# Routed feed-forward block: two plain indexed writes and a gather in place of one adding write per row

## The chip, the cores and the metric

The kernel runs on one core of a Trainium2 chip. The metric is the device time of one execution in microseconds. Before the change, three runs gave 889.02, 889.24 and 949.13 us; the median is 889.24.

## The reference, cut to what matters

One layer over four sequences of 512 tokens with 256 values each. First a conditioned feed-forward block and an attention with 16 heads on one shared key and value; their result is added to the input. Then a per-sequence mixed linear map and a routed feed-forward block with eight experts, again added:

```python
x = x + attn(cond(x, cond_8, ...), ...)
x = x + ffn(cond2(x, cond_8, ...), w_router, wi, wo)

def ffn(x, w_router, wi, wo):                       # x as 8 groups of 256 tokens
    dispatch, combine = _routing(xg, w_router)      # a token goes to its 2 best of 8 experts,
                                                    # at most 128 rows per group and expert
    expert_in = einsum('gth,gtec->gech', xg, dispatch)
    h = gelu(einsum('gech,ehf->gecf', expert_in, wi))
    expert_out = einsum('gecf,efh->gech', h, wo)
    out = einsum('gech,gtec->gth', expert_out, combine)   # weighted by the router's probability
```

So an output row is the residual of its token plus up to two expert rows, each times its probability. All arithmetic is in 32-bit floats.

## The kernel before

**Stages.** Weights of the conditioned block are gathered by row index and applied; attention runs as a software pipeline over 64 steps (16 per sequence); the pieces of the finished sequence before it (`finish`) are put between the steps one by one. The pieces of `finish(b)` end with the routing: `out` adds the attention's result to the input, giving the residual `r`, and writes it to `out_rows` (L435); `mix` makes the rows `x3` that the experts read; `choose` takes each token's two best experts; `places` gives every chosen row its place in a table `xp` in device memory, sorted by expert, and writes the rows there by eight indexed DMAs per sequence (L570), 32 in all. A row of `x3` and `xp` carries 256 values and four numbers more: the token number plus one (zero in a row that nobody filled), the first choice's expert, and both probabilities. `xp` is filled with zeros once, near the start (L199).

**The routed stage.** The last stage runs over 39 tiles of 128 rows of `xp` (`NTILE`), as many as the eight experts can need with their last tiles partly filled. Small VectorE operations work out the expert of each tile (`texp`) and its first row. The loop over tiles issues, per turn: `up(t)`, `fetch_in(t + 3)`, `turn(t + 1)`, `put(t - 1)`, `fetch_out(t + 2)`.

- `fetch_in` loads on SP's queue the tile's rows, `xt` (four buffers, L662), and the expert's first weights, `wi` (1 MB, three buffers, L671). `fetch_out` loads the second weights, `wo` (1 MB, three buffers, L675).
- `turn` transposes the rows on TensorE into PSUM (L681) and VectorE copies them to `xT` (L683).
- `up` multiplies by `wi` (L691, 32 matmul instructions in the profile); ScalarE applies the gelu (L695).
- `put` multiplies by `wo` (L704, 16 instructions) into one PSUM bank `po`. VectorE works out each row's weight and the row of the output that it belongs to, `at` (L712 to L718; a row that nobody filled goes to one of 128 spare rows behind the output), scales the row into `y` (L720), and POOL issues an indexed DMA that adds `y` to those rows of `out_rows` (L721).

**What sets the order.** The order on each engine is the order of the program; no planner moves instructions. Waits come from a dependency tracker: a reader waits for the writer of what it reads, a writer for the readers and the writer of what it overwrites. Two DMAs on `out_rows` count as conflicting, so each L721 waits for the L721 before it. Buffers in turn (`at`, `w0`, `w1` and `y` have two each) make a write wait for the last reader two tiles earlier, and for `at` and `y` that reader is a DMA. A tile's `xt` buffer is free when its last reader on VectorE is done. The rows of `xp` are declared free of conflict among themselves ("rows"); the first load of `xt` waits for all 32.

Of the kernel before, what the change touches and what calls it, by code (L numbers as in the profile page):

```python
# [9 lines left out]
F32 = mybir.dt.float32  # L10
I32 = mybir.dt.int32
AF = mybir.ActivationFunctionType
ALU = mybir.AluOpType
# [3 lines left out]
P = 128  # L17
B = 4
T = 512
NT = B * T  # L20
D = 256
NE = 8
# [4 lines left out]
CAP = 128  # L27
# [2 lines left out]
NCH = NT // P  # L30
EROWS = NG * CAP
NTILE = 2 * NCH + NE - 1
XROW = D + 4
WROW = 3 * 1024 + 10


# [1 line left out]
def adaln_attn_ffn_kernel(  # L38
# [22 lines left out]
    nc = tc.nc  # L61
# [33 lines left out]
    rows = const.tile([P, B], I32, name="rows")  # L95
    top = const.tile([P, B], F32, name="top")
    first = const.tile([P, B, NE], F32, name="first")
# [22 lines left out]
    for b in range(B):  # L120
# [3 lines left out]
            out=w,  # L124
            out_offset=None,
            in_=wcond,
            in_offset=bass.IndirectOffsetOnAxis(ap=rows[:, b : b + 1], axis=0),
# [6 lines left out]
    def load(ap, shape, name):  # L134
# [22 lines left out]
        out=upto, in_=ones, compare_op=ALU.is_ge, fill=0.0, base=0,  # L157
# [6 lines left out]
        out=sel, in_=sel, compare_op=ALU.not_equal, fill=1.0, base=-HD,  # L164
# [5 lines left out]
    for hg in range(4):  # L170
        nc.gpsimd.affine_select(
            out=spread, in_=spread, compare_op=ALU.not_equal, fill=1.0, base=-32 * hg,
            pattern=[[-1, 4], [0, 32]], channel_multiplier=1,
        )
    def numbers(name, shape, pattern, base, step):
        t = const.tile(shape, F32, name=name)
        nc.gpsimd.iota(
            t, pattern=pattern, base=base, channel_multiplier=step,
            allow_small_or_imprecise_dtypes=True,
        )  # L180
        return t


    token1 = numbers("token1", [P, NCH], [[P, NCH]], 1, 1)
    spare1 = numbers("spare1", [P, 1], [[0, 1]], NT + 1, 1)

    free = numbers("free", [P, NE], [[EROWS, NE]], 0, 0)
    begin = numbers("begin", [P, NE, NG], [[EROWS, NE], [P, NG]], 0, 0)
# [197 lines left out]
    def finish(b):  # L386

        s = seqs[b]
# [30 lines left out]
        def out(cc):  # L419

            def piece():
                if cc == 0:
                    s["r"] = rp.tile([P, 4, D], F32, name="r", bufs=1)
                px = bank(psC, "psC")
                for n in range(2):
                    for hg in range(4):
                        mm(  # L427
                            px[:, ts(n, D)], s["attn"][:, hg, ts(2 * cc + n, P)], wo_sb[:, hg, :],
                            start=hg == 0, stop=hg == 3,
                        )  # L430
                r2 = s["r"][:, ds(2 * cc, 2), :]
                nc.vector.tensor_tensor(
                    r2, px.rearrange("p (n d) -> p n d", n=2), s["x"][:, ds(2 * cc, 2), :], ALU.add
                )
                nc.sync.dma_start(  # L435
                    out_rows[ds(b * T + 2 * cc * P, 2 * P), :].rearrange("(n p) d -> p n d", p=P),
                    r2,
                )
            return piece
# [13 lines left out]

        def mix(cc):
            def piece():
                if cc == 0:
                    s["x3"] = rp.tile([P, 4, XROW], F32, name="x3")
                px = bank(psC, "psC")
                for n in range(2):
                    for c in range(2):  # L460
                        mm(
                            px[:, ts(n, D)], s["rT"][:, c, ts(2 * cc + n, P)], wb[:, c, :],
                            start=c == 0, stop=c == 1,
                        )
                nc.vector.tensor_tensor(
                    s["x3"][:, ds(2 * cc, 2), 0:D], px.rearrange("p (n d) -> p n d", n=2),
                    bias2_sb.unsqueeze(1).to_broadcast([P, 2, D]), ALU.add,
                )
            return piece

        def small(name, shape=(P, 4, NE)):
            return rp.tile(list(shape), F32, name=name)
# [4 lines left out]
        def choose():  # L477

            pl = bank(psC, "psC")
            for ch in range(4):  # L480
                for c in range(2):
                    mm(
                        pl[:, ts(ch, NE)], s["x3T"][:, c, ts(ch, P)], wr_sb[:, c, :],
                        start=c == 0, stop=c == 1,
                    )
            lg = pl[:, 0 : 4 * NE].rearrange("p (c e) -> p c e", c=4)
            rev_b = rev.unsqueeze(1).to_broadcast([P, 4, NE])
            m = small("m", (P, 4))
            nc.vector.tensor_reduce(m, lg, AX.X, ALU.max)
            pr = small("pr")  # L490
            nc.vector.tensor_tensor(pr, lg, over_experts(m), ALU.subtract)
            nc.scalar.activation(pr, pr, AF.Exp)
            sm = small("sm", (P, 4))
            nc.vector.tensor_reduce(sm, pr, AX.X, ALU.add)
            nc.vector.reciprocal(sm, sm)
            nc.vector.tensor_tensor(pr, pr, over_experts(sm), ALU.mult)

            hot = small("hot", (P, 2, 4, NE))
            top2 = small("top2", (P, 2, 4))
            left = pr  # L500
            for k in range(2):
                mk = small(f"mk{k}", (P, 4))
                nc.vector.tensor_reduce(top2[:, k], left, AX.X, ALU.max)  # L503
                eq = small(f"eq{k}")
                nc.vector.tensor_tensor(eq, left, over_experts(top2[:, k]), ALU.is_equal)
                nc.vector.tensor_tensor(eq, eq, rev_b, ALU.mult)
                nc.vector.tensor_reduce(mk, eq, AX.X, ALU.max)
                nc.vector.tensor_tensor(hot[:, k], rev_b, over_experts(mk), ALU.is_equal)
                if k == 0:
                    left = small("left")  # L510
                    nc.vector.scalar_tensor_tensor(
                        left, hot[:, 0], -4.0, pr, ALU.mult, ALU.add
                    )
                    nc.vector.tensor_scalar(
                        s["x3"][:, :, D + 1], mk, -1.0, float(NE), ALU.mult, ALU.add
                    )
            nc.gpsimd.tensor_copy(s["x3"][:, :, D], token1[:, ts(b, 4)])
            nc.gpsimd.tensor_copy(  # L518
                s["x3"][:, :, D + 2 : D + 4], top2.rearrange("p k c -> p c k")
            )  # L520
            s["hot"] = hot

        def places():
# [30 lines left out]
            for k in range(2):  # L554
# [5 lines left out]
            nc.vector.tensor_reduce(to, at, AX.X, ALU.add)  # L560
            nc.vector.scalar_tensor_tensor(to, pos, -1.0, to, ALU.add, ALU.add)

            nc.vector.tensor_scalar(
                pos, pos, float(CAP), float(2 * NE * EROWS), ALU.is_gt, ALU.mult
            )
            to_i = rp.tile([P, 2, 4], I32, name="to_i")
            nc.vector.tensor_tensor(to_i, pos, to, ALU.add)
            for ch in range(4):
                for k in range(2):
                    i = nc.gpsimd.indirect_dma_start(  # L570
                        out=xp,
                        out_offset=bass.IndirectOffsetOnAxis(ap=to_i[:, k, ch : ch + 1], axis=0),
                        in_=s["x3"][:, ch, :],
                        in_offset=None,
                        bounds_check=NE * EROWS - 1,
                        oob_is_err=False,
                    )

                    tc.declare_no_dep(i.ins, group="rows", reason="disjoint rows")
                    tc.add_to_no_dep_group("rows", i.ins)  # L580
                    scatters.append(i)
# [118 lines left out]
    def put(t):  # L700

        po = bank(psA, "psA")
        for fc in range(F // P):
            mm(  # L704
                po[:, 0:D], hT_of[t][:, fc, :], wo_of[t][:, fc, :],
                start=fc == 0, stop=fc == F // P - 1,
            )
        xt = xt_of[t]
        number, e0, p0, p1 = (xt[:, D + k : D + k + 1] for k in range(4))
        te = texp[:, t : t + 1]  # L710
        w0 = fp.tile([P, 1], F32, name="w0")
        nc.vector.tensor_scalar(w0, e0, te, p0, ALU.is_equal, ALU.mult)  # L712
        w1 = fp.tile([P, 1], F32, name="w1")
        nc.vector.tensor_scalar(w1, e0, te, p1, ALU.not_equal, ALU.mult)
        nc.vector.tensor_tensor(w0, w0, w1, ALU.add)
        nc.vector.tensor_scalar(w1, number, 0.0, spare1, ALU.is_equal, ALU.mult)
        at = fp.tile([P, 1], I32, name="at")
        nc.vector.scalar_tensor_tensor(at, number, -1.0, w1, ALU.add, ALU.add)  # L718
        y = fp.tile([P, D], F32, name="y")
        nc.vector.tensor_scalar(y, po[:, 0:D], w0, None, ALU.mult)  # L720
        nc.gpsimd.indirect_dma_start(  # L721
            out=out_rows,
            out_offset=bass.IndirectOffsetOnAxis(ap=at, axis=0),
            in_=y,
            in_offset=None,
            compute_op=ALU.add,
        )

    for t in range(3):
        fetch_in(t)  # L730
# [93 lines left out]
```

## Time and profile before

| | us |
|---|---|
| Median of three runs | 889.24 |
| The profiled execution, its own time | 960.87 |
| Its span, first to last instruction | 959.2 |
| TensorE matmuls, busy | 825.7 (86%) |
| TensorE weight loads, busy | 510.3 (53%) |
| VectorE, busy | 335.0 (35%) |
| ScalarE, busy | 245.7 (26%) |
| POOL, busy | 122.7 (13%) |
| Mean granted TensorE clock | 0.917 |
| Second `up` of the routed stage begins | 604.09 |
| Last `up` begins | 932.69 |

The profile is one execution, 71.6 us longer than the median run. Times in it are from the start of the span. Busy time on TensorE is modelled and overlaps with its weight loads, so 86% doesn't say that TensorE is the bound; which wait ends last in a stage does. DMA transfers don't count as busy time of the engine that issues them; their time to landing is from issue to the completion that others wait for. Row counts and operand names are the program's.

### The profile page before, as it was taken

To read this page: it belongs to the slowest core of one execution; us is meant where nothing else is said; L and a number is where in the kernel's file an instruction comes from. 1 tells how busy PE (TensorE), PEld (TensorE's weight loads), DVE (VectorE), ACT (ScalarE), POOL (GpSimd) and SP (SyncE) were. 2 spreads that over 40 slices of the span, in tenths; PEclk is the share of its full clock that TensorE was granted. 3 is DMA by queue.
4 is the path that set the end of the run, shared out by engine and by line. 5 is a ranking of instruction groups with operands and counts; after the bars stand their busy time and mean duration, and the time that the engine had idled before them with its cause. 6 is when DMAs were issued, how large, how long until landed. Compare 5 with 4: busy or idle time off the path is not lost. (4 is left out here: it accounts for less than half of the span.)

```text
span 959.2 us, 11458 instructions
## 1 busy us (share of the span) xinstructions
PE 825.7 (86%) x4382; PEld 510.3 (53%) x4382; DVE 335.0 (35%) x768; ACT 245.7 (26%) x417; POOL 122.7 (13%) x121
## 2 busy tenths in 40 slices
PE   2999999998999879989999781999978787887883
PEld 1444543332344433444343471999967686877772
DVE  0137464553645427565542322222111111112121
ACT  0222235445334343443344010111111110111110
POOL 4300100000000210004000303111111111111112
PEclk9999969999799799997799585999999999899997
DMA  8970100000010000101000104998777777767772
GB/s 325 338 211 0 44 1 1 1 1 0 1 45 1 34 12 12 33 1 45 1 23 1 44 23 158 384 322 295 254 241 248 247 261 234 260 233 243 252 243 26
DMA packets 39687, 122.24 MB, mean 127 GB/s; under 512 B 4432, under 2 KB 25168, under 8 KB 29136
## 3 DMA queue, kind: packets, MB, share of 16 engines
q1 hardware_dynamic: 31904, 105.81, 31.4%
q0 software_dynamic: 7728, 15.69, 6.4%
q8 instruction: 35, 0.57, 0.2%
q14 instruction: 20, 0.16, 0.1%
HBM read 101.36 MB, written 20.12 MB: 127 GB/s over the span
## 5 line engine op out<-in xcount | busy, mean ns | idle before, releaser
L339 DVE TENSOR_REDUCE negm<-psA 128x1 f32<-128x512 f32 x256 | 162.4, 684 | 123.0 <-PE psA L365 115.6
L691 PE MATMUL psA<-xT,wi_sb 128*128 128x128 f32 x1248 | 161.9, 292 | 46.6 <-DVE xT L683 44.0
L366 ACT ACTIVATE e<-psA 128x512 f32<-128x512 f32 x256 | 140.3, 595 | 198.3 <-PE psA L365 189.5
L691 PEld LDWEIGHTS psA<-xT,wi_sb 128*128 128x128 f32 x1248 | 156.8, 207 | 57.6 <-DVE xT L683 54.0
L365 PE MATMUL psA<-qs,k 32*128 32x512 f32 x512 | 183.8, 688 | 0.9 <-DVE qs L354 0.9
L335 PE MATMUL psA<-k,q 32*128 32x512 f32 x512 | 153.6, 698 | 0.0
L704 PE MATMUL psA<-wo_sb,hT 128*128 128x256 f32 x624 | 141.0, 379 | 0.0
L695 ACT ACTIVATE hT<-psA 128x512 f32<-128x512 f32 x78 | 46.6, 597 | 321.5 <-PE psA L691 321.5
L704 PEld LDWEIGHTS psA<-wo_sb,hT 128*128 128x128 f32 x624 | 115.6, 190 | 14.1
L721 POOL DMA_INDIRECT out_dram<-y,at x39 | 60.8, 1559 | 302.3 <-DVE y L720 234.3
L335 PEld LDWEIGHTS psA<-k,q 32*128 32x128 f32 x512 | 48.3, 201 | 81.3 <-issue 55.1
L718 DVE SCALAR_TENSOR_TENSOR at<-xt,w 128x1 int32<-128x1 f32 x39 | 6.2, 159 | 226.5 <-DMA out_dram<-y,at 226.2
L377 PE MATMUL psC<-e,v 128*32 128x512 f32 x512 | 74.6, 657 | 0.2 <-issue 0.2
L365 PEld LDWEIGHTS psA<-qs,k 32*128 32x128 f32 x512 | 57.1, 195 | 31.0 <-DVE negm L339 13.9
L518 POOL COPY x<-top 128x8 f32<-128x8 f32 x4 | 0.9, 218 | 389.5 <-DVE top L503 389.5
L248 PE MATMUL psA<-xT_sb,w 128*128 128x512 f32 x64 | 32.0, 624 | 17.5 <-DMA w<-in_wcond_dram,rows 17.5
L570 POOL DMA_INDIRECT xp<-x,to_i x32 | 31.8, 995 | 52.1 <-DVE negm L339 23.9
L377 PEld LDWEIGHTS psC<-e,v 128*32 128x32 f32 x512 | 10.5, 111 | 51.8 <-issue 36.7
L296 PE MATMUL psC<-coT,wq_sb 128*128 128x512 f32 x64 | 33.1, 650 | 4.6 <-ACT q L297 3.6
L683 DVE COPY xT<-psC 128x256 f32<-128x256 f32 x39 | 16.3, 417 | 53.6 <-PE psC L681 53.6
L427 PE MATMUL psC<-wo_sb,attn 128*128 128x256 f32 x128 | 31.9, 407 | 3.1 <-DVE qs L354 2.9
L253 DVE SCALAR_TENSOR_TENSOR hid<-psA,w,sg 128x512 f32<-128x512 f32 x16 | 12.0, 749 | 59.7 <-PE psA L250 59.7
(127 smaller groups left out, 593.6 us busy)
## 6 DMA issues: line engine op xcount, KB each, us to landing
wi_sb<-in_wi_dram SPq DMA_DIRECT2D x39, 1024.0 KB, 5.5
wo_sb<-in_wo_dram SPq DMA_DIRECT2D x39, 1024.0 KB, 8.3
xp<-zeros SPq DMA_DIRECT2D x1, 8450.0 KB, 31.9
xt<-xp SPq DMA_DIRECT2D x39, 130.0 KB, 2.1
xT_sb<-in_xT_dram SPq DMA_DIRECT2D x4, 512.0 KB, 7.2
w_sb<-in_w_dram SPq DMA_DIRECT2D x8, 256.0 KB, 20.2
x<-in_xtok_dram SPq DMA_DIRECT2D x4, 512.0 KB, 4.0
out_dram<-r SPq DMA_DIRECT2D x8, 256.0 KB, 2.2
```

Of the source, the lines that this page charges most:

```text
L248: mm(pu, wu[:, c, ts(hc, P)], xT_sb[:, c, ts(b, T)], start=c == 0, stop=c == 1)
L296: mm(pq, wq_sb[:, c, i, :], coT[:, c, ts(b, T)], start=c == 0, stop=c == 1)
L335: mm(pm, q[32 * j : 32 * j + 32, ds((4 * hg + hh) * P, P)], k[32 * j : 32 * j + 32, :], start=True, stop=True,)
L339: nc.vector.tensor_reduce(nm[:, hh, j, HD : HD + 1], pm, AX.X, ALU.max, negate=True)
L365: mm(ps, k[rows_j, ts(sc, P)], qs_of[u][rows_j, :], start=True, stop=True)
L366: nc.scalar.activation(e_of[n][:, :, j, :], ps.rearrange("p (h n) -> p h n", h=4), AF.Exp)
L377: mm(pa_of[u][32 * hh : 32 * hh + 32, :], seqs[b]["v"][:, sc, :], e[:, hh].rearrange("p j n -> p (j n)"), start=sc == 0, stop=sc == 3,)
L427: mm(px[:, ts(n, D)], s["attn"][:, hg, ts(2 * cc + n, P)], wo_sb[:, hg, :], start=hg == 0, stop=hg == 3,)
L691: mm(ph[:, ts(n, P)], wi_of[t][:, c, ts(4 * half + n, P)], xT_of[t][:, c, :], start=c == 0, stop=c == 1,)
L695: nc.scalar.activation(hT_of[t][:, ds(4 * half, 4), :].rearrange("p f t -> p (f t)"), ph, AF.Gelu_apprx_tanh,)
L704: mm(po[:, 0:D], hT_of[t][:, fc, :], wo_of[t][:, fc, :], start=fc == 0, stop=fc == F // P - 1,)
L721: nc.gpsimd.indirect_dma_start(out=out_rows, out_offset=bass.IndirectOffsetOnAxis(ap=at, axis=0), in_=y, in_offset=None, compute_op=ALU.add,)
```

## The change

In place of one adding write per tile, a tile makes three indexed DMAs on `out_rows` that only move data.

- A token's *first* row is the one whose expert has the lower number (its tile comes earlier), or its only row if the other found no place. Its *second* row is the other. `places` works out for both choices whether they are first (`early`) and stores two more numbers per row: the token number plus one where the choice is first, else zero.
- The rows of `x3` and `xp` also carry the residual: they grow from 260 to 518 values. `r` now lies in `x3`; the residual is still written to `out_rows` by the unchanged DMA of `out`.
- In `put`, VectorE works out the weight and two lists of rows, for first and for second rows; entries that don't apply point past the end and are skipped. A gather (`was`) fetches the output rows of the tile's second rows; `y` is the weighted row plus the residual and is written to the first rows; `y2` is the weighted row plus `was` and is written to the second rows.
- Order: gather `g(t)` waits for the write of first rows `f(t - 1)`, by a dependency set by hand. Writes of first rows, writes of second rows and gathers are declared free of conflict among themselves and with each other, apart from that one wait. `was` has two buffers, filled with zeros ahead of the stage.
- The output loses its 128 spare rows.

```diff
-XROW = D + 4
+META = 6
+XROW = 2 * D + META
+NOROW = 2.0 * NE * EROWS
...
-                    s["r"] = rp.tile([P, 4, D], F32, name="r", bufs=1)
+                    s["x3"] = rp.tile([P, 4, XROW], F32, name="x3")
+                    s["r"] = s["x3"][:, :, D + META : XROW]
...
+            early = small("early", (P, 2, 4))
+            for k in range(2):
+                nc.vector.tensor_tensor(
+                    early[:, k], s["mk"][k], s["mk"][1 - k], ALU.is_gt
+                )
+                nc.vector.tensor_tensor(early[:, k], early[:, k], pos[:, 1 - k], ALU.add)
+                nc.vector.scalar_tensor_tensor(
+                    s["x3"][:, :, D + 4 + k], early[:, k], 1.0, token1[:, ts(b, 4)],
+                    ALU.min, ALU.mult,
+                )
...
-        number, e0, p0, p1 = (xt[:, D + k : D + k + 1] for k in range(4))
+        number, e0, p0, p1, a0, a1 = (xt[:, D + k : D + k + 1] for k in range(META))
...
-        nc.vector.tensor_scalar(w1, number, 0.0, spare1, ALU.is_equal, ALU.mult)
-        at = fp.tile([P, 1], I32, name="at")
-        nc.vector.scalar_tensor_tensor(at, number, -1.0, w1, ALU.add, ALU.add)
+        def by_rank(v0, v1, name):
+            a = fp.tile([P, 1], F32, name=name)
+            nc.vector.tensor_scalar(a, e0, te, v0, ALU.is_equal, ALU.mult)
+            b = fp.tile([P, 1], F32, name=name + "b")
+            nc.vector.tensor_scalar(b, e0, te, v1, ALU.not_equal, ALU.mult)
+            nc.vector.tensor_tensor(a, a, b, ALU.add)
+            return a
+
+        def index(a, name):
+            none = fp.tile([P, 1], F32, name=name + "n")
+            nc.vector.tensor_scalar(none, a, 0.0, NOROW, ALU.is_equal, ALU.mult)
+            i = fp.tile([P, 1], I32, name=name)
+            nc.vector.scalar_tensor_tensor(i, a, -1.0, none, ALU.add, ALU.add)
+            return bass.IndirectOffsetOnAxis(ap=i, axis=0)
+
+        weight = by_rank(p0, p1, "weight")
+        a = by_rank(a0, a1, "a")
+        rest = fp.tile([P, 1], F32, name="rest")
+        nc.vector.tensor_tensor(rest, number, a, ALU.subtract)
+        first, second = index(a, "first_i"), index(rest, "second_i")
+        bounds = dict(bounds_check=NT - 1, oob_is_err=False)
+        was = was_of[t % 2]
+        g = nc.gpsimd.indirect_dma_start(
+            out=was, out_offset=None, in_=out_rows, in_offset=second, **bounds
+        )
+        free_of(g, "second", "was")
+        tc.add_to_no_dep_group("was", g.ins)
+        if t > 0:
+            tc.add_manual_dep(
+                g.ins, first_of[t - 1].ins.name,
+                mybir.DependencyInfo(mybir.DependencyClass.Sync, mybir.DependencyReason.DATA),
+                reason="the first rows of earlier tiles",
+            )
         y = fp.tile([P, D], F32, name="y")
-        nc.vector.tensor_scalar(y, po[:, 0:D], w0, None, ALU.mult)
-        nc.gpsimd.indirect_dma_start(
-            out=out_rows,
-            out_offset=bass.IndirectOffsetOnAxis(ap=at, axis=0),
-            in_=y,
-            in_offset=None,
-            compute_op=ALU.add,
-        )
+        nc.vector.scalar_tensor_tensor(
+            y, po[:, 0:D], weight, xt[:, D + META : XROW], ALU.mult, ALU.add
+        )
+        f = nc.gpsimd.indirect_dma_start(
+            out=out_rows, out_offset=first, in_=y, in_offset=None, **bounds
+        )
+        free_of(f, "first", "second", "was")
+        tc.add_to_no_dep_group("first", f.ins)
+        first_of[t] = f
+        y2 = fp.tile([P, D], F32, name="y2")
+        nc.vector.scalar_tensor_tensor(y2, po[:, 0:D], weight, was, ALU.mult, ALU.add)
+        i = nc.gpsimd.indirect_dma_start(
+            out=out_rows, out_offset=second, in_=y2, in_offset=None, **bounds
+        )
+        free_of(i, "first", "second", "was")
+        tc.add_to_no_dep_group("second", i.ins)
```

In the changed file the copy to `xT` is L694, `up`'s matmuls are L702, the gather is L747, `y` is L759, the write of first rows L762, `y2` L769 and the write of second rows L770.

More of the change, by code (lines that the diff above doesn't have):

```diff
@@ L184, in adaln_attn_ffn_kernel @@
     token1 = numbers("token1", [P, NCH], [[P, NCH]], 1, 1)
-    spare1 = numbers("spare1", [P, 1], [[0, 1]], NT + 1, 1)
     free = numbers("free", [P, NE], [[EROWS, NE]], 0, 0)
@@ L455, in piece @@
             def piece():
-                if cc == 0:
-                    s["x3"] = rp.tile([P, 4, XROW], F32, name="x3")
                 px = bank(psC, "psC")
@@ L499, in choose @@
             top2 = small("top2", (P, 2, 4))
+            s["mk"] = []
             left = pr
@@ L502, in choose @@
                 mk = small(f"mk{k}", (P, 4))
+                s["mk"].append(mk)
                 nc.vector.tensor_reduce(top2[:, k], left, AX.X, ALU.max)
@@ L561, in places @@
             nc.vector.scalar_tensor_tensor(to, pos, -1.0, to, ALU.add, ALU.add)
-            nc.vector.tensor_scalar(
-                pos, pos, float(CAP), float(2 * NE * EROWS), ALU.is_gt, ALU.mult
-            )
+            nc.vector.tensor_scalar(pos, pos, float(CAP), NOROW, ALU.is_gt, ALU.mult)
             to_i = rp.tile([P, 2, 4], I32, name="to_i")
             nc.vector.tensor_tensor(to_i, pos, to, ALU.add)
+            early = small("early", (P, 2, 4))
[8 more added lines that the diff above has]
+                )
             for ch in range(4):
@@ L708, in put @@
         xt = xt_of[t]
-        number, e0, p0, p1 = (xt[:, D + k : D + k + 1] for k in range(4))
+        number, e0, p0, p1, a0, a1 = (xt[:, D + k : D + k + 1] for k in range(META))
         te = texp[:, t : t + 1]
[L711 to L715, printed above, removed]
@@ new lines, in put, with free_of @@
+        i = nc.gpsimd.indirect_dma_start(
[3 more added lines that the diff above has]
+        tc.add_to_no_dep_group("second", i.ins)
+    first_of = {}
+    was_of = []
+    for n in range(2):
+        t = fp.tile([P, D], F32, name=f"was{n}", bufs=1)
+        nc.gpsimd.memset(t, 0.0)
+        was_of.append(t)
+    def free_of(i, *groups):
+        for g in groups:
+            tc.declare_no_dep(i.ins, group=g, reason="disjoint rows")
@@ L817 @@
         )
-    args.append(nc.dram_tensor("out_dram", (NT + P, D), F32, kind="ExternalOutput").ap())
+    args.append(nc.dram_tensor("out_dram", (NT, D), F32, kind="ExternalOutput").ap())
     with tile.TileContext(nc) as tc:
@@ L822 @@
     out = np.asarray(r.results[0]["out_dram"])
-    return np.ascontiguousarray(out[:NT]).reshape(B, T, D)
+    return out.reshape(B, T, D)
```

## The prediction

> **What bounds the kernel now.** I read the chain that ended last first, then its pieces in order of time, the waits behind it, the landing times of the transfers, and last the busy time by stage. The chain, by engine and by line:
>
> ```profile
> DMA 28%; DVE 2%; issue 1%; POOLq 0%; DVEq 0%
> DMA out_dram<-y,at 28%; DVE y L720 1%; DVE at L718 1%; POOLq L819 0%; DVEq L718 0%; DVE xT L683 0%; POOLq L721 0%
> ```
>
> It starts at 660.87 us and is almost wholly the adding scatter of L721. Two turns from its middle and one from its end (start, length, what):
>
> ```profile
> 776.73 8.67 DMA out_dram<-y,at
> ...
> 785.50 0.16 DVE at L718
> 785.66 0.41 DVE y L720
> ...
> 786.16 8.36 DMA out_dram<-y,at
> ...
> 941.62 3.82 DMA out_dram<-y,at
> ```
>
> Every scatter starts when the one before has landed: all add into the same rows, so each is ordered behind the last. The waits say the same from the other side (waiter, releaser: total us, times, longest):
>
> ```profile
> DVE at L718 <- DMA out_dram<-y,at: 226.2, 31, 8.6
> ```
> ```profile
> PE psA L691 <- DVE xT L683: 44.0, 25, 2.8
> ```
>
> VectorE stands at `at` until an old scatter frees its index buffer, the copy xT queues behind it, and TensorE waits for xT. From the start of the second `up` at 604.09 to the last at 932.69, 37 tiles took 8.88 us each. Without that wait TensorE needs less: while the scatters were still catching up, its tiles began at 640.21, 647.46 and 654.70, every 7.25 us. Median landing times (last figure, us):
>
> ```profile
> wi_sb<-in_wi_dram SPq DMA_DIRECT2D x39, 1024.0 KB, 5.5
> wo_sb<-in_wo_dram SPq DMA_DIRECT2D x39, 1024.0 KB, 8.3
> ...
> xt<-xp SPq DMA_DIRECT2D x39, 130.0 KB, 2.1
> ...
> out_dram<-y,at POOLq DMA_INDIRECT x39, 8.7
> ...
> xp<-x,to_i POOLq DMA_INDIRECT x32, 2.5
> ```
>
> The adding scatter takes 8.7 beside 2 MB of weights and 3.8 when none are left (941.62); a plain scatter with little beside it takes 2.5. And the DMA engines, where the period was 7.25 (the row's last three figures are clock, DMA share, GB/s):
>
> ```profile
> 610.00:662.00 52.00, 52.00 (x358) 48.95 (x357) 12.62 (x49) 8.36 (x14) 10.55 (x7) 1.00 0.97 333
> 662.00:930.00 268.00, 225.74 (x1446) 205.78 (x1445) 45.50 (x195) 34.63 (x58) 42.48 (x28) 0.96 0.74 248
> ```
>
> There they were 97% busy: right behind the scatter chain stand TensorE at 7.25 and the DMA engines at almost the same.
>
> **What the Trainium skill says.** "DMA: Bandwidth & Descriptors", section "Queues, rings and completion order": each DMA engine takes its queues in turn, a packet at a time. The trace agrees that weights lengthen a scatter (8.7 against 3.8) without stopping it: at 97% load the scatters of 612.91, 620.67, 627.62, 635.52 and 642.69 still followed each other in 7.0 to 7.9. The same page, "Anatomy of one DMA": a fixed cost near 2 us, mostly the receipt of the write. The plain scatter's 2.5, of which 0.98 is POOL, fits. "Perfetto Trace Analysis", section "DMA Instruction — SWDGE (GPSIMD)": POOL's interval is only the writing of descriptors, so 1.56 on POOL and 8.7 to land don't conflict. No page prices an adding DMA against a plain one.
>
> **The change, part by part.** Working on the profiled execution, 960.87 us with a span of 959.2.
>
> *Removed:* the order of all scatters behind each other. *Put in its place:* the gather g(t) waits for the first-rows scatter f(t-1); the second-rows scatter s(t) waits only for its data.
>
> *POOL:* three issues a tile for one. A plain indexed issue is 0.98 and 0.3 between two, so 3.9 us a tile of 7.25: hidden, and it would show only beyond 7.25. In its order g, f, s, s(t) holds g(t+1) back, but y2, which s needs, comes before g's index on VectorE anyway.
>
> *VectorE:* eleven small operations where five took 1.09 us (608.53 to 609.62); at the same spacings of 0.18 to 0.30, 2.5 us. y keeps about 0.48 and a second y2 adds 0.48. New is that y2 waits for the gather, and behind it queue the next xT (for which TensorE waits), the next indices (for which POOL waits) and y. The loop is xT 0.41, indices 2.5, hand-overs 0.2, the landing of g, y2 0.48: 3.6 + Lg. At Lg = 2.5 it is 6.1, under TensorE's 7.25; it meets 7.25 at 3.65 and today's 8.88 at 5.3.
>
> *Lg* is not in the trace. From below: 2.5, the plain scatter. From above: loaded, the adding scatter took 7.0 to 7.9 against 3.8, so the load adds up to 4.1, and 6.6 in all. I take 3.0 to 3.7. Reason: the fetch of a tile's rows (xt) now waits for y(t), its last reader, and the weights queue behind it on SP; g(t) is issued just before y(t). The traffic of a tile therefore starts after the gather, and what the gather meets is the tail of the tile before. Early tiles moreover gather nothing: "first" is the lower expert, so the first experts' tiles are all first rows, the last ones' all second.
>
> *Lf*, the landing of f(t), holds g(t+1): a period of 1.1 + Lf. Bounds again 2.5 and 6.6: 3.6 to 7.7, at 6.2 no bound. s has no one behind it but the buffers of two tiles later.
>
> *SP:* xt leaves after y(t) and not after the index, 2.4 us later (645.86 against 648.3), and wi behind it. wi has three buffers: it then lands by about 659 for an `up` at 661.9. Hidden; a period longer than 7.25 only adds room.
>
> *DMA load per tile:* weights 2.10 MB, xt 2072-byte rows 0.265 (was 0.133), and 4096 written plus 2048 read rows over 39 tiles, 0.16 MB (was 0.13, and added into). 2.52 MB at the 333 GB/s of the stage that was 97% full is 7.6 us; at the 384 GB/s of 600 to 624, 6.6. I take 7.6, slightly over TensorE.
>
> *Before the stage:* xp doubles, so its zero fill goes from 31.9 to about 64 us, from 35 to 99 us; the next load on SP leaves at 100.4 and its data are needed at 268. Hidden, also if it ran 100 us longer. Six small operations of 0.17 to 0.2 per sequence hide behind TensorE for three sequences and cost about 1.2 ahead of the last eight row scatters; with wider rows to fetch, 1.5 us.
>
> *The end:* TensorE stops at 943.44, the span ends 15.8 later, since four scatters were still in line. After: the last `put` but one, y and y2 1.0, indices 2.5, g 2.5, y2 0.6, s 2.5, the same 4.8 after it, less the 3.6 of the last `put`: 10.3. Gain 5.5.
>
> *Sum:* 37 x (7.6 - 8.88) = -47.4, end -5.5, start +1.5: -51.4 us. Against the profiled execution 909. The median of the runs is 889.24; they lie 71.6 lower. The granted clock explains some 43 of it, in 96 to 576 us (one minus the clock of each 24 us slice, times TensorE's busy time), where the change has no part. The scatter chain doesn't run at that clock, so I carry the saving over in us: **838**.
>
> **Rivals.**
> (a) *TensorE or the DMA engines set the pace*, 7.25 to 7.9: 37 x 7.25 saves 60.3, 37 x 7.9 saves 36.3, with -4 for start and end 825 to 849. For it: 97% at 7.25. My forecast, 0.62.
> (b) *The gather shows in part*, Lg 4.5 to 5 and periods of 8.1 to 8.6, about 865. For it: DMA would be over 85% full, so the gap before the next weights is short. 0.13.
> (c) *A load cost, not an adding cost*: f is issued together with the weights as the old scatter was and lands in nearly 8, since the load and not the adding made the 8.7; g(t+1) waits for it, 1.1 + 7.8 = 8.9, about 886: the change swaps one chain for another. Against it: a scatter that only moves was 1.3 faster even unloaded. 0.08.
> (d) *Slower*: VectorE blocked at y2 by a gather among weights. If it always meets the full load, Lg is 6.6 and the period 10.2: 37 x 1.32 - 4 = +45, 934. It decides from Lg 5.3 on. For it: `was`, unlike the old scatter, has VectorE and with it TensorE directly behind it. Against it: such a period leaves the DMA engines idle a quarter of the time, and that idle time lies just where g runs. 0.17.
>
> **How the numbers follow.** About 2% is what a measurement of this kernel can tell from no change: 871 to 907. Faster: (a) and most of (b), 0.73; the rest of (b) and (c) are the same, 0.10; slower is (d), 0.17. The predicted time is that of (a). The range starts at 820, a little under (a)'s lower end for a DMA rate above 333 GB/s, and reaches over (b) to (c) at 892; (d) is left out.
>
> **What would show it.** After: no chain of one transfer; the chain should run through TensorE or weights landing. `up` every 7.3 to 7.9 us, DMA share above 0.9 between 662 and the last tiles, landing of the gather under 4 us, VectorE's wait for it short and none of TensorE's for xT. Wrong if VectorE's wait at y2 (L769) totals over 100 us with landings beyond 5 (then d or b), if POOL's gather (L747) waits for f landing in about 8 (c), or if wi lands late and L702's matmuls wait for it, which would put the DMA load above 7.9.

## The result and the profile after

The changed kernel takes **955.19 us** (median of four runs, 951.69 to 956.45); the kernel before, in the same comparison, 895.49. The ratio is **1.069, with a 95% interval of 1.060 to 1.079**: slower by 7%, where 838 us had been forecast, in a range of 820 to 892. A second comparison (e1) gave 1.080 (1.073 to 1.086).

One thing must be said about the kernel before, or no number below can be understood: most of its executions take 877 to 897 us (called ordinary below), some take longer, up to 961, and the profile that the prediction read (960.87 us) was one of the long kind.

The profile of the changed kernel has a span of 954.8 us. Its chain that ended last, by engine and by line:

```profile
issue 17%; DMA 16%; POOL 5%; POOLq 0%
DMA out_dram<-y,first_i 16%; POOL was L747 2%; POOL out_dram L762 2%; POOL out_dram L770 1%; POOL xp L581 0%; POOLq L762 0%; POOLq L878 0%; POOLq L747 0%; POOLq L770 0%; POOL was L780 0%
```

The adding scatter is gone from the chain, and a plain one stands in its place: the write of first rows, `first_i`. The waits of VectorE, TensorE and POOL in the same profile, from 560 us on (waiter, releaser: total us, times, longest):

```profile
DVE y L769 <- DMA was<-out_dram,second_i: 214.2, 39, 9.6
```
```profile
PE psA L702 <- DVE xT L694: 45.1, 20, 3.8
```
```profile
POOL out_dram L770 <- DVE y L769: 118.9, 34, 5.9
POOL was L747 <- DMA out_dram<-y,first_i: 39.0, 13, 4.9
```

VectorE's wait of 226 us at `at` has become one of 214 us at `y2`, and TensorE waits for xT as long as before (45 us against 44). From the second `up` at 601.30 to the last at 934.92 a tile takes 9.02 us, where the profile of the prediction had 8.88. Against that profile the change is a tie; against the ordinary execution of before it costs about 65 us.

That ordinary execution is seen in another profile of the unchanged kernel (e5 below, span 882.5 us). Its chain, and its stretch from 662 to 850 us, to be held against the same stretch of the changed kernel below it (length, then busy us of TensorE, its weight loads, VectorE, ScalarE, POOL; granted clock, DMA share, GB/s):

```profile
PE 32%; DMA 1%; POOL 0%; issue 0%; POOLq 0%; DVE 0%; SPq 0%
```
```profile
662.00:850.00 188.00, 188.00 (x1299) 177.26 (x1298) 46.93 (x182) 31.04 (x52) 40.22 (x27) 1.00 0.98 328
```
```profile
662.00:850.00 188.00, 161.19 (x1036) 148.82 (x1037) 60.97 (x294) 24.48 (x41) 63.87 (x63) 0.95 0.75 278
```

In its ordinary execution the kernel before keeps TensorE busy throughout the stage, at 7.25 us a tile, and the DMA engines 98% busy: there was nothing to be had from its scatters. The changed kernel leaves a seventh of the stretch empty on TensorE and a quarter on the DMA engines. The difference of the two spans, 72.3 us, is 37 x (9.02 - 7.25) = 65.5 in the stage, 8.0 more ahead of its second `up` (this start varies from 588 to 607 us among profiles of kernels that are alike there), and 1.2 less at the end.

### The profile page after: what moved, and what is told of

Read it like the earlier page. It is cut to its first block, busy times and chain, and to the rows that moved or that the text cites. A ratio compares the mean times of both kernels' runs of the same rounds, so it can differ in the third digit from the quotient of the medians.

```text
span 954.8 us, 12068 instructions
## 1 busy us (share of the span) xinstructions
PE 826.2 (87%) x4382; PEld 514.1 (54%) x4382; DVE 386.9 (41%) x1065; ACT 245.6 (26%) x417; POOL 181.1 (19%) x200
## 5 line engine op out<-in xcount | busy, mean ns | idle before, releaser
L702 PE MATMUL psA<-xT,wi_sb 128*128 128x128 f32 x1248 | 165.1, 296 | 47.3 <-DVE xT L694 45.1
L702 PEld LDWEIGHTS psA<-xT,wi_sb 128*128 128x128 f32 x1248 | 160.1, 210 | 57.9 <-DVE xT L694 54.8
L366 PE MATMUL psA<-qs,k 32*128 32x512 f32 x512 | 180.9, 680 | 3.0 <-ACT e L367 2.0
L769 DVE SCALAR_TENSOR_TENSOR y<-psA,weight,was 128x256 f32<-128x256 f32 x39 | 18.9, 484 | 214.2 <-DMA was<-out_dram,second_i 214.2
L770 POOL DMA_INDIRECT out_dram<-y,second_i x39 | 38.5, 987 | 139.7 <-DVE y L769 118.9
L747 POOL DMA_INDIRECT was<-out_dram,second_i x39 | 40.9, 1049 | 92.1 <-DMA out_dram<-y,first_i 39.0
L762 POOL DMA_INDIRECT out_dram<-y,first_i x39 | 39.2, 1005 | 12.4 <-issue 11.7
```

The costliest lines, as they stand in the source:

```text
L366: mm(ps, k[rows_j, ts(sc, P)], qs_of[u][rows_j, :], start=True, stop=True)
L702: mm(ph[:, ts(n, P)], wi_of[t][:, c, ts(4 * half + n, P)], xT_of[t][:, c, :], start=c == 0, stop=c == 1,)
L747: g = nc.gpsimd.indirect_dma_start(out=was, out_offset=None, in_=out_rows, in_offset=second, **bounds)
L762: f = nc.gpsimd.indirect_dma_start(out=out_rows, out_offset=first, in_=y, in_offset=None, **bounds)
L770: i = nc.gpsimd.indirect_dma_start(out=out_rows, out_offset=second, in_=y2, in_offset=None, **bounds)
```

## The experiments

### e1: the changed kernel again

No edit.

> The changed kernel once more, beside the kernel before, to see whether the difference of the medians belongs to the routed stage. In the two profiles that stage is alike (37 tiles at 9.02 us after, at 8.88 before) and the granted clock too (0.914 and 0.917), yet the medians differ by 60 us. Theory 1, the clock: the kernel before has runs with a higher granted clock in its first 576 us, and the changed kernel differs from it by under 1% (5 to 10 us) wherever the clock is the same; then times of before near 890 come with a clock of about 0.97 and those near 955 with 0.92. Theory 2, the change itself: at the same clock the changed kernel is 40 to 60 us longer, and its unprofiled runs spend it somewhere the profile doesn't show.

Measured: 958.81 us (955.24 to 968.3) against 890.08, ratio 1.080. Both theories missed. The clock was not it. From 100 to 576 us, ahead of the routed stage, it is 0.90 in the profile of the prediction, 0.89 in the changed kernel and 0.90 in the ordinary execution of e5 (third figure from the right in these three rows, in this order):

```profile
100.00:576.00 476.00, 439.80 (x2247) 195.89 (x2245) 230.10 (x420) 182.00 (x315) 34.58 (x36) 0.90 0.05 16
100.00:576.00 476.00, 436.15 (x2245) 195.88 (x2243) 235.47 (x455) 181.93 (x315) 34.57 (x36) 0.89 0.06 23
100.00:576.00 476.00, 432.61 (x2243) 193.82 (x2241) 235.12 (x441) 181.73 (x315) 39.62 (x41) 0.90 0.05 17
```

Nor does the changed kernel hide anything: its profile shows the time that its runs take. It was the profile of before that stood for something else.

### e5: the kernel before under the profiler again

No edit.

> The kernel before once more under the profiler. Its profiled execution took 960.87 us and showed 8.88 us a tile, while its median is 889 to 890; a version without the gather (e4) took 889 too, at 7.25 us a tile and with TensorE on the chain. Theory 1: the ordinary execution of before is already at TensorE's 7.25 a tile, and the profiled one fell behind its scatters; then a profile near 890 shows 7.25 to 7.4 a tile and no wait of VectorE for a scatter, and a profile near 960 shows the 8.9 of before again. Theory 2: before runs at 8.9 a tile always and something ahead of the routed stage is 70 us shorter at 890.

Measured: 885.86 us, ratio 0.999 (0.997 to 1.002), and this time a profiled execution of 884.24. Theory 1 holds: 7.25 us a tile, and VectorE never waits for a scatter. Landing times in this profile:

```profile
wi_sb<-in_wi_dram SPq DMA_DIRECT2D x39, 1024.0 KB, 6.9
...
out_dram<-y,at POOLq DMA_INDIRECT x39, 6.3
```

In the profile of the prediction these were 5.5 and 8.7. In the ordinary execution the weights stream without a gap (98%) and an adding scatter takes 6.3 beside them. The scatters still stand in line behind each other, and POOL waits for the one before:

```profile
POOL out_dram L721 <- DMA out_dram<-y,at: 160.7, 29, 7.7
```

From the last completion of one to the start of the next pass 0.75 us, so a scatter needs about 7.0, just inside 7.25, and nothing behind POOL waits for it. In the long kind the load stops and starts (74%), each burst of weights starts with a scatter, and that scatter takes 8.7.

### e8: the kernel before with more buffers

```diff
-        w0 = fp.tile([P, 1], F32, name="w0")
+        w0 = fp.tile([P, 1], F32, name="w0", bufs=4)
...
-        at = fp.tile([P, 1], I32, name="at")
+        at = fp.tile([P, 1], I32, name="at", bufs=4)
...
-        y = fp.tile([P, D], F32, name="y")
+        y = fp.tile([P, D], F32, name="y", bufs=4)
```

`w1` likewise.

> The kernel before with four buffers in place of two for at, y and the two weights, so that VectorE waits for a scatter four tiles back and not two. Theory 1: in the profiled execution of before the scatters fall behind once and then, through VectorE, hold back xt and the weights, which start together with the scatter and keep it slow; with more buffers the slip isn't passed on, and profile and median both lie at 885 to 895. Theory 2: the scatters by themselves can't keep 7.25 under that load: the buffers only put the lag off by two tiles, 8.7 to 8.9 a tile, near 955 in the profiled execution.

Measured: 884.85 us, ratio 0.999 (0.997 to 1.002); 20 runs from 876.19 to 888.79, where the kernel before, in the same session, has 10 of 55 above 920. In its profile three scatters in a row, of tiles 4 to 6, take 8.6 to 9.2 us, as long as in the long kind, and `up` still comes every 7.25 us. So theory 1 holds: the lag of a scatter reaches TensorE through the two buffers of `at` and `y`. It is no faster at the median, since there TensorE is the bound, but none of its 20 executions is of the long kind. What makes the first scatter fall behind isn't shown.

### e2: a scatter that doesn't add

```diff
             in_=y,
             in_offset=None,
-            compute_op=ALU.add,
         )
```

This leaves out the sum: each row overwrites.

> The kernel before, with the adding left out of the scatter: the rows are overwritten, the order of the scatters stays. Theory 1, the weights beside it make a scatter slow: it lands in 7 to 8 us, POOL's part being 0.57 shorter, and a tile takes 7.9 to 8.5 us, so the stage ends 15 to 35 us earlier. Theory 2, the adding makes it slow (the prediction's view): it lands in 5 to 5.5 us, TensorE and the DMA engines set 7.3 to 7.6 us a tile, 48 to 58 us less.

Measured: 888.65 us, ratio 0.998 (0.995 to 1.001), 7.25 us a tile. As TensorE is the bound, the time decides nothing; the landing times of this profile do:

```profile
wi_sb<-in_wi_dram SPq DMA_DIRECT2D x39, 1024.0 KB, 6.3
```
```profile
out_dram<-y,at POOLq DMA_INDIRECT x39, 6.4
```

The view's 6.4 is the median of the four scatters whose landing it could tell; the completion records of the trace give 6.4 for all 39 as well. Beside the weights, a scatter that only moves its rows thus lands after 6.4 us, the adding one of e5 after 6.3, though POOL spends 0.97 on it and not 1.56. **Beside the weights, adding cost nothing that can be seen at the landing.** It does without them: the last three scatters, with no load left, took 2.4 here and 3.7 to 3.8 in e5. Neither forecast of the landing was met (7 to 8, or 5 to 5.5), but theory 2, the prediction's view that adding makes the loaded scatter slow, falls.

### e4: the new order without the gather

```diff
-        g = nc.gpsimd.indirect_dma_start(
-            out=was, out_offset=None, in_=out_rows, in_offset=second, **bounds
-        )
...
-        nc.vector.scalar_tensor_tensor(y2, po[:, 0:D], weight, was, ALU.mult, ALU.add)
+        nc.vector.tensor_scalar(y2, po[:, 0:D], weight, None, ALU.mult)
         i = nc.gpsimd.indirect_dma_start(
-            out=out_rows, out_offset=second, in_=y2, in_offset=None, **bounds
+            out=out_rows, out_offset=second, in_=y2, in_offset=None,
+            compute_op=ALU.add, **bounds
         )
...
+        if t > 0:
+            tc.add_manual_dep(
+                i.ins, first_of[t - 1].ins.name,
...
```

> The changed kernel without the gather: first rows are written plainly with the residual, second rows are added by an adding scatter that waits for the first rows of the tile before; the scatters of second rows don't wait for each other. Nothing is left out of the computation. If only the order of the DMAs set the pace, two tiles need 7.6 + 1.9 = 9.5 us on POOL, 4.8 a tile, and TensorE or the DMA engines at 7.3 to 7.7 take over: 45 to 55 us less than the kernel before at the same clock. If the load on the DMA engines is the bound in itself (more bytes a tile), 8.5 us or more a tile and under 15 us gained.

Measured: 889.22 us, ratio 1.000 (0.997 to 1.002), 7.25 us a tile. TensorE took over as expected, at the lower end; the gain of 45 to 55 us did not exist, since before was there already. The experiment also prices a large part of the change at nothing: doubled rows of `xp` and its zero fill, the extra small operations, two indexed writes in place of one, all are in e4. What is left to explain the 65 us is the gather and the waits around it.

### e7: the changed kernel without the load

```diff
     def fetch_in(t):
...
+        if t >= 3:
+            wi_of[t] = wi_of[t - 3]
+            return
         wi_of[t] = wexp.tile([P, 2, F], F32, name="wi_sb")
```

`fetch_out` likewise. Tiles from the fourth on use weights of other experts.

> The changed kernel loading the experts' weights for the first three tiles only (later tiles reuse them, so the computation is another). Theory 1, the transfers are slow because of the weights beside them: first rows and gather land in 2.5 to 3 us, VectorE's loop is 6.1 to 6.6, TensorE sets 7.25, 885 to 890 us. Theory 2, three dependent indexed DMAs cost as much without any load: no change, about 955.

Measured: 885.18 us, ratio 1.000 (0.997 to 1.002), 7.25 us a tile. Landing times in its profile:

```profile
was<-out_dram,second_i POOLq DMA_INDIRECT x39, 2.7
out_dram<-y,first_i POOLq DMA_INDIRECT x39, 2.7
```

The same three dependent DMAs, on the same POOL and VectorE, cost nothing when the weights are away. So it is their landing under load.

### e3 and e6: one wait at a time

e3 issues y2 and the second write one turn later:

```diff
         first_of[t] = f
+        todo[t] = (po, weight, was, second)
+
+    def second_rows(t):
...
             put(t - 1)
+            if t > 1:
+                second_rows(t - 2)
...
```

The weights and the two index lists get three buffers for it in place of two.

> The changed kernel with y2 and the write of the second rows issued one turn of the loop later, so that VectorE no longer stands at y2 for a gather issued a moment before. Theory 1, the chain is landing of the first rows, then gather: POOL's gather still waits for f, 1.35 + 7.6 = 9.0 us a tile, no change against the changed kernel. Theory 2, VectorE's stand at y2 sets the pace: 7.4 to 7.7 us a tile, some 50 us less.

e6 takes the wait for the first rows away, by gathering from other data:

```diff
-            out=was, out_offset=None, in_=out_rows, in_offset=second, **bounds
+            out=was, out_offset=None, in_=other, in_offset=second, **bounds
         )
...
-        if t > 0:
-            tc.add_manual_dep(
-                g.ins, first_of[t - 1].ins.name,
...
```

> The changed kernel with its gather reading another tensor of the same shape (so its sums for second rows are not the model's), and hence without the wait for the first rows of the tile before; VectorE still stands at y2. Theory 1, the pace of 9.0 needs both waits in one loop (two tiles: 1.35 + f 7.6 + gather 6.4 + 3.0 on VectorE): without f's wait the gather leaves ahead of the weights and lands in about 4, VectorE's loop is 3.6 + 4.0 = 7.6, so 890 to 905 us. Theory 2, the gather's landing among the weights is enough: 3.6 + 5.5 or more, 9 us a tile, about 955.

Measured: e3 takes 904.41 us (four runs, 888.95 and three from 903.51 to 906.5, one of these profiled; without a ratio), 7.38 a tile in its profile; e6 takes 902.93 us, ratio 1.015 (1.005 to 1.025), 7.84 a tile. In e3 theory 1 had said no change at all, and it falls: the wait for first rows does not make 9.0 by itself. In e6 theory 2 falls: the stand at y2 does not either. Each edit alone takes away more than 50 us, so the 9.0 needs both in one loop. In e6's profile VectorE still waits long at y2, TensorE hardly:

```profile
DVE y L761 <- DMA was<-other,second_i: 174.8, 39, 7.6
```
```profile
PE psA L702 <- DVE xT L694: 13.8, 11, 3.1
```

What e6 still loses comes late. Its first eight tiles or so keep 7.25, its last 18 need 8.3 each: with later experts the gathers fetch more rows and land later (in e9, where no gather is held back, 3.6 to 5.5 us for the first five, which fetch no row, and 5.7 to 5.8 for three that fetch all 128).

The loop can be read in the changed kernel's own timeline. POOL's DMAs over two tiles (start, length on POOL, what, in brackets the idle time before and what ended it):

```profile
766.59 1.05 POOL L747 DMA_INDIRECT was<-out_dram,second_i  x1 [1.17 <-DVE second_i L737]
767.94 1.01 POOL L762 DMA_INDIRECT out_dram<-y,first_i  x1 [0.31 <-issue]
771.33 0.99 POOL L770 DMA_INDIRECT out_dram<-y,second_i  x1 [2.38 <-DVE y L769]
775.62 1.05 POOL L747 DMA_INDIRECT was<-out_dram,second_i  x1 [3.30 <-DMA out_dram<-y,first_i]
776.98 1.01 POOL L762 DMA_INDIRECT out_dram<-y,first_i  x1 [0.30 <-issue]
782.76 0.99 POOL L770 DMA_INDIRECT out_dram<-y,second_i  x1 [4.77 <-DMA out_dram<-y,first_i]
784.91 1.05 POOL L747 DMA_INDIRECT was<-out_dram,second_i  x1 [1.17 <-DVE second_i L737]
```

(The label of 782.76 names first rows; that write needs only y2, which had ended at 782.48.) VectorE in the same stretch:

```profile
770.57 0.48 DVE L769 SCALAR_TENSOR_TENSOR y<-psA,weight,was 128x256 f32<-128x256 f32 x1 [3.86 <-DMA was<-out_dram,second_i]
...
773.13 0.48 DVE L759 SCALAR_TENSOR_TENSOR y<-psA,weight,xt 128x256 f32<-128x256 f32 x1
782.00 0.48 DVE L769 SCALAR_TENSOR_TENSOR y<-psA,weight,was 128x256 f32<-128x256 f32 x1 [8.39 <-DMA was<-out_dram,second_i]
782.40 0.41 DVE L694 COPY xT<-psC 128x256 f32<-128x256 f32 x1
```

and the loads that SP issues:

```profile
766.74 0.33 SPq L673 DMA_DIRECT2D xt<-xp  x1
767.31 0.55 SPq L682 DMA_DIRECT2D wi_sb<-in_wi_dram  x1
...
773.64 0.33 SPq L673 DMA_DIRECT2D xt<-xp  x1
774.21 0.33 SPq L682 DMA_DIRECT2D wi_sb<-in_wi_dram  x1
```

The gather of 766.59 leaves just ahead of the weights and lands in 4.0. y at 773.13 frees xt, and the next weights start. But the next gather, whose indices are ready by 773.2, must wait for the first rows of 767.94, which were sent among the weights before. Their last completion comes after 6.9, at 774.82, and POOL's gather starts 0.8 later, at 775.6: 7.7 in all. So it goes out into the new burst, takes 6.4, and all that time VectorE stands at y2 with xT behind it. Then the indices take their turn, 2.9 from y2 to the next gather at 784.91. In all 1.35 + 7.7 + 6.4 + 2.9 = 18.3 us for two tiles.

### e9: both edits

> Both edits together: y2 and the second write one turn later (e3, 904 us) and the gather reading another tensor, without the wait for first rows (e6, 903 us; sums of second rows are not the model's). Theory 1, the changed kernel's pace comes from one loop with two waits, and each of e3 and e6 leaves the other wait standing, which costs the 15 us that remain: 884 to 890, TensorE at 7.25 a tile. Theory 2, the 15 us are the greater traffic and the three issues a tile on POOL: 900 to 905 again.

Measured: 885.79 us, ratio 1.002 (1.000 to 1.005), 7.25 a tile, with TensorE on the chain:

```profile
PE 32%; DMA 1%; POOL 1%; issue 0%; DVE 0%; POOLq 0%; SPq 0%
```

Theory 1: with both waits out of the loop the whole difference is gone, with all the traffic and all three issues on POOL still there (the sums of second rows are not the model's here). Not all that e3's profile has over the ordinary execution is its other wait, though: of 21.1 us, 5.0 lie in the stage, all in its last ten tiles, and 13.5 ahead of its second `up`. That start, 606.75, is the latest of all profiles (the others lie between 588 and 604), its cause isn't known, and e3's shortest run took no longer than the kernel before.

### e10: six buffers for xt

```diff
-        xt_of[t] = fp.tile([P, XROW], F32, name="xt", bufs=4)
+        xt_of[t] = fp.tile([P, XROW], F32, name="xt", bufs=6)
```

> The changed kernel with six buffers for xt in place of four: the fetch of a tile's rows, and the weights queued behind it on SP, no longer wait for y of the tile before. Theory 1a, first rows and gather are slow because the weights start together with them (in the kernel before a scatter lands in 8.7 when it starts with the weights and in 6.3 when the weights run on without a gap): the loads spread, first rows and gather land in 5.5 to 6.5, 7.8 to 8.3 us a tile, 915 to 935 us. Theory 1b, it is only that weights are there, whenever they start: the loop stays near 9.0 a tile, 950 to 960.

Measured: 923.79 us, ratio 1.043 (1.028 to 1.057), 8.38 a tile. The time lies in the range of theory 1a, and the fetch of xt and weights that waits for y is shown to cost 0.64 of the 1.77 us a tile, between a third and a half of the loss.

The mechanism that 1a gave for it is borne out in part. First rows land hardly sooner: after 6.1 us at the median and not 6.3, by the completion records of the two traces. But fewer gathers are held back. Of the 35 gathers that meet weights (tiles 1 to 35), 17 start over 1 us after their index list in the changed kernel, and land after 6.4 at the median, the other 18 after 4.5; in e10 only 6 start so late. (The profile names first rows as the end of POOL's wait at the gather 13 times in the changed kernel and 4 times here. It leaves some cases out in both: a gather that starts 0.8 after the last completion of first rows is put down to y, which it doesn't need, when y ended within these 0.8 us.) Why the hold gets shorter when the loads spread stays open.

## Why the prediction was wrong

**The base.** This is the step that failed first. Of the 117 us between forecast and measurement it has 51, the saving that wasn't there; the other 66 are the next two steps, and they make the sign. The prediction took 8.88 us a tile for the pace of the kernel before, had the ordinary runs 71.6 us shorter than the profile, gave "some 43 of it" to the clock and carried the saving "over in us" to 889. The clock at TensorE was not it. The numbers for a better reading were on the page: TensorE's own pace of 7.25, which the prediction quoted, is 1.63 us a tile or 60 us less over 37 tiles, and that is most of the gap between profile and median. (Between the profiles of before and e5, 76.7 us apart, 60 lie in the stage, 11 ahead of its second `up`, 5 at the end.) The term "37 x (7.6 - 8.88) = -47.4" had nothing to be taken from: its true size against the median is nought, as e4 and e9 show by reaching 7.25 and saving nothing.

**Lf, the landing of the first rows.** Put between 2.5 and 6.6, for a period of 1.1 + Lf, and called no bound up to 6.2. From their issue to the gather that waited for them it took 7.4 at the median (the 13 cases that the profile names, 7.1 to 8.9): 6.6 to the last completion, the top of the range, and 0.8 more until POOL started the gather, which the prediction put at nothing. The 1.1 measured 1.35. The top of the range came from adding scatters less what adding was supposed to cost, and beside weights adding costs nothing at the landing (e2): the 7.0 to 7.9 from the start of one loaded scatter to the next, which hold the wait on POOL too, should have been taken as they stood.

**Lg, the landing of the gather.** "3.0 to 3.7", because it leaves ahead of the weights. About every other tile it does, and lands after 4.5. The other goes out after its weights, since it had waited for the first rows, and takes 6 to 7. The prediction treated the wait for f and VectorE's stand at y2 as two bounds, of which the larger counts; in truth one fed the other, and e3, e6 and e9 show that the 9.0 needs both. Also, that early tiles "gather nothing" was no help: the first five gathers fetch no row (their packets in e7's trace hold 4 or 16 bytes), and in the changed kernel they took 3.6 to 8.1 us all the same.

**What held.** The zero fill, the wider rows, the small operations and nearly the whole load of 2.5 MB a tile are free or fit: e4 has them and runs at 7.25 with the DMA engines 97% busy. POOL's three issues a tile fit as well: e9 has them and runs at 7.25. VectorE's loop holds in form, but its fixed part measured 2.9 (from y2 to the next gather in e6) and not 3.6: with 5.0 from gather to y2, e6's mean, that is 7.9, against 7.84 a tile. The end came out shorter than in the profile of before, 19.9 us from the last `up` against 26.5, as forecast near 21; the ordinary execution has 21.1, so of that gain too only 1.2 is real.

**The rivals.** (c) had the right cause of slow first rows, load and not adding, but on the wrong base called it no change. That its period, 8.9, is nearly the 9.02 measured is luck: it counted the wait for first rows in every tile and no stand at y2, and with that wait alone e3 runs at 7.38. (d) named the right place, VectorE at y2 with TensorE behind it, and the right sign, with a price of 10.2 a tile where 9.02 was measured. It took every gather to meet the full load, where about half of them do. The two were held apart and are one loop.

## What to carry to other kernels

Before an edit is priced, check that the profiled execution is the one that the runs are made of: if it is longer than the median, look for a stage whose excess over its next bound is about that gap, before any is given to the clock. A transfer whose landing an engine waits for is priced under the load that starts with it, whatever it computes on the way. And when two new waits lie on one loop, follow it through two turns with times; the larger of two separate bounds is not the answer, and moving either the consumer one turn later or the dependency elsewhere opens the loop.

## What the runs showed of the hardware

- An indexed DMA of 128 rows that adds lands as late as one that only moves, beside the same weights: 6.3 us (e5) and 6.4 (e2). With no weights left beside them the last three of each took 3.7 to 3.8 and 2.4.
- The same adding scatter lands sooner beside weights that stream without a gap at 98% (6.3, e5) than beside bursts of 74% that start with it (8.7, the profile of the prediction).
- Between the last completion of an indexed DMA and the start of the next one on POOL that waits for it pass 0.75 us (e5) to 0.8 (the changed kernel).
- A gather all of whose 128 indices lie out of bounds saves little with no weights beside it: about 2.2 us in four of the first five of e7 (3.8 in the other), against 2.8 to 2.9 for the three that fetch 128 rows. Beside weights it saves more: a median of 4.0 for the first five of e9 against 5.7 to 5.8.
